# Two-layer graph network in fp32: W2 asked for behind x on one queue, adj of batch 2 handled within O of batch 1, the product WqWk in pieces of 128 columns

## The chip, the cores and the metric

The kernel runs on one core of a Trainium2 chip. The metric is the device time of one execution in microseconds (us), as a median of several executions. All timed executions here are marked as of the fast state, and only those are compared; one kernel was run once, and its state is unknown. The engines are called PE (tensor engine), PEld (its weight loads), DVE (vector engine), ACT (ScalarE), POOL (GpSimd) and SP (the engine that issues most of the DMAs). An *eviction* is the copy of a finished product out of PE's result memory; until it is done, the next product of the same buffer waits. The *granted clock* is the share of its full clock that PE was given.

## The reference

There are 32 independent batches of 512 x 512 fp32, with two layers. Cut to what matters:

```python
h = relu(layernorm(x))                                  # layer 0
agg = (adj @ h) / max(rowsum(adj), 1e-6)
x = x + relu(concat([h, agg]) @ W.T)                    # W = [W1 | W2]
h = relu(layernorm(x))                                  # layer 1
q, k = split(h @ Wqk); v = h @ Wv
w = (q * (adj @ (k * mask))).sum(-1) * mask / sqrt(512)
x = x + softmax(w)[:, :, None] * v
```

## The kernel before

Every product of 512 x 512 is done with seven block products (m1 to m7) in place of eight, and needs sums of blocks of both operands beforehand, on DVE. The products of a batch are y = h W2, o = h W1 + adj y (added to x), u = adj h1, t = h1 (Wq WkT), whose row sums with u give the softmax's scores, and v = h1 Wv. PE runs them in stages of 14 block products; O(1) is the stage of o of batch 1, and y(1)/u(0) the one that mixes y of batch 1 with u of batch 0. A stage has a *plan*: at each of its steps, other work is put behind the step's matmuls on the other engines. DVE and ACT keep to the order in which their instructions stand, so that one that waits holds up those behind it: in the trace before, ACT's scaling of adj waited 3.29 us, and the eviction behind it came at 100.41, while PE stood waiting for it.

```python
def multiply(d):                      # WqWk, once, between O of batch 0 and y(1)/u(0)
    p = held["m", d] = mm_tile(f"pm_{d}")
    for a in range(C):
        nc.tensor.matmul(p.rearrange("p a f -> p (a f)"), wqT[:, a, ts(d, P)], held["wkT"][:, a, :],
                         start=(a == 0), stop=(a == C - 1))
```

adj has to be scaled by its row sums and turned. It goes through DRAM: `sum` and `write` are ACT's, `degrees` is DVE's, `read` is a DMA that exchanges blocks, and `turn` is DVE's transpose of blocks of 32 x 32.

```python
class FrontA:
    def sum(self, c):      # ACT: row sums
        nc.scalar.activation(v, v, AF.Copy, accum_out=DEG[self.b][:, c:c + 1])
    def degrees(self, h):  # DVE: max and reciprocal
        ...
    def write(self, c):    # ACT scales, then a DMA to DRAM
        nc.scalar.activation(v, v, AF.Copy, scale=self.rdeg[:, c:c + 1])
        nc.sync.dma_start(out=self.to.d[c], in_=v)
class Turned:
    def read(self, h):     # four DMAs back from DRAM
    def turn(self, h):     # DVE transposes
    def sums(self, i):     # DVE: left sums of blocks
```

The start, and the plan of O of batch 0 as far as it turns the mask:

```python
def start():
    load_x(0)                                            # SP queue
    s2 = [exchange(weight_source(w0[:, F:2 * F])[8 * h:8 * h + 8], f"sw2_{h}", queue=nc.scalar) for h in range(2)]
    fa.load(0); fa.load(1)                               # adj of batch 0
    s1 = exchange(...)                                   # W1
    fh.load(0); sq = exchange(...); sk = exchange(...)   # x of batch 1, Wq, Wk
    ...                                                  # cut: layer norm of batch 0, y(0)
    fh.load(1); fb.load(0)                               # x and adj of batch 1
    nc.sync.dma_start(out=mask_sb, in_=nodemask)
    ...
    at(2, mask_order)                                    # DVE reorders the mask
    at(3, mask_turn)                                     # PE transposes it (pmk)
    at(4, mask_keep)                                     # ACT keeps it
```

## Time and profile before

| kernel before | value |
|---|---|
| time, median of 6 executions | 2382.48 us (2381.6 to 2383.76) |
| span of the profiled execution | 2380.0 us |
| PE busy | 99% |
| PE idle before its first instruction | 17.2 us |
| other PE waits of more than 0.15 us | 4, together 9.5 us, all between 97 and 148 us |

A PE that is 99% busy leaves 1% in question, and nearly all of that lies in the first 160 us. So the page's averages say little, and the timelines of these 160 us say nearly everything. They are shown in the prediction. Only the lines that are needed later for a comparison stand here. They are from the timelines of DVE (first) and PE (second; start, duration, instruction, count, and in brackets the idle time before it and what ended it):

```profile
11.49 0.69 DVE L221 BATCH_NORM_STATS2 st<-x 128x6 f32<-128x512 f32 x1 [10.63 <-DMA x<-in_x_dram]
```

```profile
17.23 1.97 PE L496 MATMUL h<-identity,h 128*128 128x128 f32 x8 [17.23 <-ACT h L533]
...
61.51 13.90 PE L645 MATMUL pm<-wkT,wqT 128*128 128x512 f32 x32
```

x is there at 11.5, PE begins at 17.2, and the product WqWk stands from 61.5 to 75.2 without a gap.

### The profile page before, as it was taken

The page shows a single profiled execution, that of the slowest core. Times are in us where ns is not written, and L with a number is a line of the kernel's source. Part 1 is how long each engine was busy: PE and PEld are TensorE (multiplying, and loading weights), DVE is VectorE, ACT ScalarE, POOL GpSimd, SP SyncE. Part 2 cuts the span into 40 slices and gives each one's busy share as a digit, 9 for nine tenths or more (in the row PEclk, how much of TensorE's full clock was granted, in tenths as well). Part 3 has the DMA queues.
Part 4 walks back from the last instruction along what each step waited for, and adds up shares of the span by engine and source line. Part 5 has one row for each costly group of instructions (what it writes and reads, how often), then busy time and mean ns, then how long its engine had stood idle before and what let it go on. Part 6 is the DMA issues. An engine that isn't in the chain of part 4 may idle for free.

```text
span 2380.0 us, 30871 instructions
## 1 busy us (share of the span) xinstructions
PE 2345.8 (99%) x10820; PEld 2056.2 (86%) x10820; DVE 1491.9 (63%) x3132; ACT 860.3 (36%) x1555; POOL 91.9 (4%) x134
## 2 busy tenths in 40 slices
PE   7999999999999999999999999999999999999998
PEld 6778888888888888888888888888888888888887
DVE  5666666666666666666666566666666666666544
ACT  4433333433333433334333334333343333343312
POOL 0000000000000000000000000000000000000000
PEclk9999999999999999999999999999999999999999
DMA  8845656456556456565465564565554565645412
GB/s 163 217 132 144 165 146 149 135 125 166 142 142 162 127 136 172 146 143 141 127 158 149 145 159 125 134 174 142 142 146 130 151 157 146 156 127 131 116 37 70
DMA packets 363596, 337.71 MB, mean 142 GB/s; under 512 B 32657, under 2 KB 266129, under 8 KB 363441
## 3 DMA queue, kind: packets, MB, share of 16 engines
q1 hardware_dynamic: 361264, 334.69, 55.8%
q10 hardware_dynamic: 2176, 1.05, 0.3%
q8 instruction: 85, 1.39, 0.3%
q14 instruction: 71, 0.57, 0.1%
HBM read 203.49 MB, written 132.12 MB: 141 GB/s over the span
## 4 chain that ended last, share of the span: by engine, by line
PE 95%; DMA 2%; DVE 1%; SPq 1%; ACT 0%; issue 0%; POOL 0%; DVEq 0%; ACTq 0%; POOLq 0%
PE pp_o L124 18%; PE pp_v L124 9%; PE pp_t L124 9%; PE pp_y L124 9%; PE pp_u L124 9%; PE pq_o L124 9%; PE pq_v L124 5%; PE pq_t L124 5%; PE pq_y L124 4%; PE pq_u L124 4%; PE pr_o L124 4%; PE pr_v L124 2%; PE pr_t L124 2%; PE pr_u L124 2%; PE pr_y L124 2%; DMA x<-in_x_dram 0%
## 5 line engine op out<-in xcount | busy, mean ns | idle before, releaser
L124 PE MATMUL pp_t<-mR,h1T 128*128 128x256 f32 x1024 | 243.8, 381 | 4.6 <-ACT t L91 4.6
L124 PE MATMUL pp_u<-h1m,aT 128*128 128x256 f32 x1024 | 242.0, 379 | 3.2 <-ACT u L91 3.2
L124 PE MATMUL pp_v<-vR,h1T 128*128 128x256 f32 x1024 | 242.0, 379 | 1.1 <-ACT v L91 1.1
L124 PE MATMUL pp_y<-w2R,hT 128*128 128x256 f32 x1024 | 243.0, 380 | 0.0
L124 PE MATMUL pp_o<-w1R,hT 128*128 128x256 f32 x1024 | 242.1, 379 | 0.5 <-ACT o L91 0.5
L124 PE MATMUL pp_o<-y,aT 128*128 128x256 f32 x1024 | 241.9, 379 | 0.0
L124 PEld LDWEIGHTS pp_t<-mR,h1T 128*128 128x128 f32 x1024 | 195.6, 191 | 31.8 <-ACT t L91 5.0
L124 PEld LDWEIGHTS pp_u<-h1m,aT 128*128 128x128 f32 x1024 | 194.5, 190 | 30.0 <-ACT u L91 3.6
L124 PEld LDWEIGHTS pp_y<-w2R,hT 128*128 128x128 f32 x1024 | 195.3, 191 | 27.1 <-issue 0.5
L124 PEld LDWEIGHTS pp_v<-vR,h1T 128*128 128x128 f32 x1024 | 194.5, 190 | 27.9 <-ACT v L91 1.5
L124 PEld LDWEIGHTS pp_o<-w1R,hT 128*128 128x128 f32 x1024 | 194.3, 190 | 27.2 <-ACT o L91 0.9
L124 PEld LDWEIGHTS pp_o<-y,aT 128*128 128x128 f32 x1024 | 194.5, 190 | 26.4
L91 ACT ACTIVATE o<-pp_o 128x512 f32<-128x512 f32 x96 | 57.3, 597 | 370.9 <-PE pp_o L124 370.9
L235 ACT ACTIVATE h1m<-x,nmr,rstd 128x512 f32<-128x512 f32 x128 | 100.0, 807 | 173.7 <-DVE nmr L231 173.7
L199 DVE STREAM_TRANSPOSE aT<-saT 128x1024 f32<-128x1024 f32 x62 | 77.2, 1245 | 130.1 <-DMA saT<-daT 102.1
L91 ACT ACTIVATE v<-pp_v 128x512 f32<-128x512 f32 x128 | 75.5, 590 | 223.3 <-PE pp_v L124 223.3
L91 ACT ACTIVATE y<-pp_y 128x512 f32<-128x512 f32 x128 | 76.4, 597 | 204.0 <-PE pp_y L124 204.0
L91 ACT ACTIVATE u<-pp_u 128x512 f32<-128x512 f32 x128 | 76.2, 595 | 140.4 <-PE pp_u L124 140.4
L227 POOL TENSOR_TENSOR rstd<-rstd,mhalf 128x4 f32<-128x4 f32 x64 | 66.6, 1040 | 1561.5 <-ACT m_o L91 879.8
L124 PE MATMUL pq_y<-w2R,hT 128*128 128x256 f32 x512 | 121.0, 379 | 0.0
L124 PE MATMUL pq_o<-w1R,hT 128*128 128x256 f32 x512 | 121.0, 379 | 0.0
L124 PE MATMUL pq_o<-y,aT 128*128 128x256 f32 x512 | 120.9, 379 | 0.0
(115 smaller groups left out, 3745.2 us busy)
## 6 DMA issues: line engine op xcount, KB each, us to landing
x<-in_x_dram SPq DMA_DIRECT2D x128, 256.0 KB, 5.8
a<-in_adj_dram SPq DMA_DIRECT2D x256, 128.0 KB, 3.1
dh1T<-h1m SPq DMA_DIRECT2D x128, 256.0 KB, 2.5
sh1T<-dh1T SPq DMA_DIRECT2D x256, 128.0 KB, 3.4
out_dram<-x SPq DMA_DIRECT2D x256, 128.0 KB, 2.3
n<-in_x_dram SPq DMA_DIRECT2D x248, 128.0 KB, 4.8
daT<-a SPq DMA_DIRECT2D x124, 256.0 KB, 2.0
dhT<-n SPq DMA_DIRECT2D x124, 256.0 KB, 2.0
```

What stands on the lines that cost most here:

```text
L91: nc.scalar.activation(o, i, AF.Copy)
L124: nc.tensor.matmul(p[:, rc, :], lt[:, LEFT[k], dk, ts(rc, P)], rt[:, RIGHT[k], dk, :], start=first and n == 0, stop=True, skip_group_check ...
L199: nc.vector.transpose(o, t.rearrange("p k (c r) -> p k c r", r=R))
L227: nc.gpsimd.tensor_tensor(rstd, rstd, mhalf, op=ALU.pow)
L235: nc.scalar.activation(o, i, AF.Relu, scale=t[1][:, c:c + 1], bias=t[2][:, c:c + 1])
```

## The change

Its intent has three parts. W2, which came over ACT's queue beside x, is asked for on SP's queue behind x, so that x comes sooner. The handling of batch 2's adj, which held DVE and ACT in the stages y(1)/u(0) and O(1), is spread over O(1), with its transposes late. WqWk is computed in pieces of 128 columns.

```diff
-        s2 = [exchange(weight_source(...)[8 * h:8 * h + 8], f"sw2_{h}", queue=nc.scalar) for h in range(2)]
+        s2 = [exchange(weight_source(...)[8 * h:8 * h + 8], f"sw2_{h}") for h in range(2)]
...
         def multiply(d):
             for a in range(C):
-                nc.tensor.matmul(
-                    p.rearrange("p a f -> p (a f)"), wqT[:, a, ts(d, P)], held["wkT"][:, a, :],
-                    start=(a == 0), stop=(a == C - 1),
-                )
+                for e in range(C):
+                    nc.tensor.matmul(
+                        p.rearrange("p a f -> p (a f)")[:, ts(e, P)], wqT[:, a, ts(d, P)],
+                        held["wkT"][:, a, ts(e, P)],
+                        start=(a == 0 and e == 0), stop=True, skip_group_check=True,
+                    )
...                                                       # stage y(1)/u(0)
-        at2(9, fc.sum, 0)
-        at2(10, fc.sum, 1)
-        at2(10, fc.degrees, 0)
-        at2(11, fc.write, 0)
-        at2(12, fc.write, 1)
         f3 = FH[3] = FrontH(3)
         at2(12, f3.load, 0)
-        at2(12, fc.to.read, 0)
-        at2(13, f3.load, 1)
...                                                       # stage O(1)
+                f, ta, th = FA[2], FA[2].to, FH[2].to
+                for h in range(2):
+                    for c in range(2):
+                        at(3 * h + c, f.sum, 2 * h + c)
+                        at(3 * h + c + 2, f.write, 2 * h + c)
+                    plan[3 * h + 2].insert(0, lambda h=h: FA[2].degrees(h))
+                    at(5 + 3 * h, ta.read, h)
+                    at(9 + 3 * h, ta.turn, h)             # before: steps 1 and 7
+                    at(10 + 3 * h, th.read, h)
+                at(4, FH[3].load, 1)
...                                                       # th.turn of batch 2: steps 3 and 4 of t(0)/v(0), before 1 and 2
...                                                       # the aT sums of batch 2 go to y(2)/u(1)
```

More of the change, by code (lines that the diff above doesn't have):

```diff
@@ L185, in half_rows, with exchange @@
         return t
-    def exchange(src, name, t=None, queue=None):
+    def exchange(src, name, t=None):
         if t is None:
@@ L192, in exchange @@
         for q in range(Q):
-            (queue or nc.sync).dma_start(out=t[q * R:(q + 1) * R, :, :], in_=src[:, :, ts(q, P)].rearrange("k r j -> r k j"))
+            nc.sync.dma_start(out=t[q * R:(q + 1) * R, :, :], in_=src[:, :, ts(q, P)].rearrange("k r j -> r k j"))
         return t
@@ L509, in start @@
         load_x(0)
-        s2 = [exchange(weight_source(w0[:, F:2 * F])[8 * h:8 * h + 8], f"sw2_{h}", queue=nc.scalar) for h in range(2)]
+        s2 = [exchange(weight_source(w0[:, F:2 * F])[8 * h:8 * h + 8], f"sw2_{h}") for h in range(2)]
         fa = FA[0] = FrontA(0)
@@ L724, in at @@
                 plan.setdefault(n, []).append(lambda: f(*args))
-            if i + 1 < B:
-                ta, th = FA[i + 1].to, FH[i + 1].to
-                n = 1 if i > 1 else 5
-                at(1, ta.turn, 0)
-                at(n + 2, ta.turn, 1)
-                at(3, th.read, 0)
-                at(n + 4, th.read, 1)
-                for k in range(4):
-                    at(n + 3 + k, ta.sums, k)
-            if i == 1:
-                for c in (2, 3):
-                    at(c - 2, FA[2].sum, c)
-                    at(c, FA[2].write, c)
-                plan[2].insert(0, lambda: FA[2].degrees(1))
-                at(3, ta.read, 1)
+            if i == 1:
+                f, ta, th = FA[2], FA[2].to, FH[2].to
[8 more added lines that the diff above has]
+                at(4, FH[3].load, 1)
                 for k in range(4):
@@ L744 @@
                     at(10 + k, F1[0].to.sums, k)
+            elif i + 1 < B:
+                ta, th = FA[i + 1].to, FH[i + 1].to
+                at(1, ta.turn, 0)
+                at(3, ta.turn, 1)
+                at(3, th.read, 0)
+                at(5, th.read, 1)
+                for k in range(4):
+                    at(4 + k, ta.sums, k)
             if i + 2 < B:
@@ L769 @@
             if i + 1 < B:
-                at(1, th.turn, 0)
-                at(2, th.turn, 1)
+                n = 1 if i > 1 else 3
+                at(n, th.turn, 0)
+                at(n + 1, th.turn, 1)
                 for k in range(4):
@@ L802 @@
             at(8, s.store, 1)
+            if i == 1:
+                for k in range(4):
+                    at(5 + k, FA[2].to.sums, k)
             t1 = F1[i].to
```

## The prediction

> **What bounds the kernel now.** I read the page first, for the bound. Then I read the tensor engine's waits, and then what lies behind each wait in the timelines of the vector engine (DVE), ScalarE (ACT) and the tensor engine (PE). The second column of a timeline is the duration, and the bracket holds the idle time before.
>
> ```profile
> PE 2345.8 (99%) x10820; PEld 2056.2 (86%) x10820; DVE 1491.9 (63%) x3132; ACT 860.3 (36%) x1555; POOL 91.9 (4%) x134
> ```
>
> PE is the bound. Nearly all its work is fp32 matmuls of 256 columns, whose instructions start every 0.216 us. From 161 us to the tail it has no recorded idle time, and the change touches nothing of the later loop passes. What can move is the start and the first 160 us, where all the waits lie:
>
> ```profile
> PE h L496 <- ACT h L533: 17.8, 2, 17.2
> PE pp_t L124 <- ACT t L91: 4.6, 1, 4.6
> PE pp_u L124 <- ACT u L91: 3.2, 1, 3.2
> PE pp_v L124 <- ACT v L91: 1.1, 1, 1.1
> PE pp_o L124 <- ACT o L91: 0.5, 1, 0.5
> ```
>
> The 17.2 us is the start: x lands (DVE's first statistics at 11.49), then the normalization, then the transposes. The other four sum to 9.5 us. Behind them stands DVE, held by the transposes of adj, and ACT behind DVE:
>
> ```profile
> 96.97 1.25 DVE L199 STREAM_TRANSPOSE aT<-saT 128x1024 f32<-128x1024 f32 x1 [3.43 <-DMA saT<-daT]
> 113.30 1.25 DVE L199 STREAM_TRANSPOSE aT<-saT 128x1024 f32<-128x1024 f32 x1 [7.36 <-DMA saT<-daT]
> 126.07 1.25 DVE L199 STREAM_TRANSPOSE aT<-saT 128x1024 f32<-128x1024 f32 x1 [5.41 <-DMA saT<-daT]
> ...
> 99.31 0.72 ACT L307 ACTIVATE a<-a,rdeg 128x512 f32<-128x512 f32 x1 [3.29 <-DVE rdeg L303]
> ...
> 115.49 1.33 ACT L307 ACTIVATE a<-a,rdeg 128x512 f32<-128x512 f32 x2 [8.35 <-DVE rdeg L303]
> ...
> 101.06 1.99 PE L124 MATMUL pp_u<-h1m,aT 128*128 128x256 f32 x8 [3.21 <-ACT u L91]
> ...
> 137.80 3.78 PE L124 MATMUL pp_t<-mR,h1T 128*128 128x256 f32 x8 [4.63 <-ACT t L91]
> ```
>
> The last two transposes of DVE are of adj of batch 2. In the first, ACT's scaling of that adj sits in front of the eviction that PE needs at 101. In the other two, DVE loses 12.8 us and reaches the h1T sums and the statistics late, so PE stands 4.63 us at 133.17. Its group at 137.80 then takes 3.78 us where its like takes 1.89:
>
> ```profile
> 120.00:140.00 20.00, 15.37 (x66) 13.08 (x66) 14.28 (x28) 4.00 (x6) 1.29 (x1) 0.92 0.45 137
> 140.00:160.00 20.00, 18.87 (x79) 15.92 (x79) 15.06 (x39) 8.86 (x15) 1.01 (x1) 0.91 0.50 143
> ```
>
> The column after POOL is the granted clock: in the trace it is 0.5 for 6.83 us from 136.68. PE ran 5.7 us of those and so lost about 2.85 us.
>
> **What the Trainium skill says.** (1) "TensorE: Matmul & The Clock Gate", Part 1 (the HAM clock gate): an idle window of about 3.4 us, free-running, halves the clock. The trace agrees: after 4.63 us idle the clock halved for 6.83 us; after 3.21 us idle it didn't. (2) The same page, LDWEIGHTS: a load costs columns / 1.2 ns, 107 ns for 128. The records show 190 ns each, but where two loads follow each other with nothing before them (44.13), they start 108 ns apart, and PEld's 0.30 us for both is 0.108 + 0.19. So 190 includes latency, and the trace agrees with 107 as occupancy. (3) "DMA: Bandwidth & Descriptors", Issuing engines are not separate DMA queues: queues share the same 16 DMA engines and interleave. The trace agrees: while x and W2 came by two queues, together they got 175 to 230 GB/s in each us from 4 to 12, no more than later loads from one queue. (4) The clock-gate page, "Architectural detail", calls ACT and DVE strict FIFO; the waits above, with evictions caught behind an unrelated adj operation, are that.
>
> **Part 1, W2 behind x.** Today x (four DMAs of 256 KB) shares the engines with W2 (1 MB in 512 B packets), and its fourth DMA is issued only at 4.73. It lands at 11.47. Alone at the front: the batch-1 x lands in steps of 1.1 us, and a first transfer of this size needs some 3.5 us (Wv: issued 54.23, landed 57.72), so 0.72 + 3.5 + 3 x 1.1 = 7.5; from the moved bytes (0.44 MB by 4 us, then 225 GB/s for 0.61 MB) 6.8. I take 7.2: x comes 4.3 us earlier. W2 needs 5.6 us after it (as W1's 1 MB did, 18.03 to 23.64) and lands at 12.8, just when DVE is through with the statistics. So y(0) starts about 4.3 us earlier, near 17.5.
>
> But the loads are saturated from 2 to 41 us, and changing their order doesn't make the sum smaller: by 13 us I count 2.28 MB moved before and 2.26 after. Last in that queue stands nodemask:
>
> ```profile
> 42.58 0.41 DVE L615 COPY mask_by<-mask 32x512 f32<-32x512 f32 x1 [1.96 <-DMA mask<-in_nodemask_dram]
> ...
> 43.77 0.43 PE L622 MATMUL pmk<-identity,mask_by 32*128 32x32 f32 x4
> ```
>
> The first line has DVE idle for the mask; PE arrives 0.74 us after DVE's copy is done (42.99 + 0.04 against 43.77). With the shift PE arrives at 39.5, waits for the mask until about 43.05, and of the 4.3 us only **0.7** are left. The gain turns into a new wait of 3.6 us. (W1 at 23.6 holds DVE for 1.8 us too, but PE meets w1R only at 32.)
>
> **Part 2, adj of batch 2 moved.** No work goes away. Two sums, a degrees step and two scalings leave the y(1)/u(0) stage; the second half's follow; the transposes move from O's steps 1 and 7 to steps 9 and 12; the four aT sums (4 x 0.6 = 2.4 us DVE) go one stage on, where DVE is busy 12 to 14 of 20 us.
>
> End of y(1)/u(0): the transpose at 96.97 (batch 1, stays) still holds DVE, but ACT no longer waits behind it: the eviction of u's c22 comes at 94.3 instead of 100.41. The **3.21** go.
>
> In O(1) I write times as after, O beginning near 99 (97.7 + 1.73, less 0.35). DVE clears its aT and y backlog at 104.5, gives the degrees at 106.0; ACT scales until 107.4; the loads in front keep the DMAs full until about 108, so the two writes land at 109.7. Then n of batch 3 is loaded (lands 113.9) and adj is read back (4 issues of 0.45, landing 116.2). DVE comes to that transpose at 115.5, so it waits 0.7 instead of 7.36. Second half: written by 116.9, read by 121.2, wanted at 122.2: no wait. DVE's work in O: 4 + 4 sums of mR and vR 4.8, finishes 4.3, statistics 3.2, transposes 2.5, h1T sums 2.4, small ones 1.0, so 18 us in a stage of 24.2. h1T's third sum is done at 124.0, PE needs it at 128.4; ACT's last normalization is done at 123.2, the first eviction of t is wanted at 125. So the waits of 0.5, 4.63 and 1.13 and the 2.85 of clock go: **9.1**. The narrowest place is v's m6 at 133.6, whose eviction stands behind a normalization that I put at 132.3: 1.3 us of slack.
>
> **Part 3, WqWk in pieces.** Before, 16 products x 2 instructions of 512 columns at 0.429 us are 13.73 us (61.51 to 75.24). After, 64 x 2 of 128 columns, each with a weight load of its own. Columns cost 0.107 + 0.0025, the load 0.107 in the shadow; transposes of 128 columns with a load each already start every 0.109. 128 x 0.1095 = 14.0, so **+0.3**, all on PE's path.
>
> **Sum**: 0.7 + 3.2 + 9.1 - 0.3 = 12.7 us off 2382.3, which gives 2369.6.
>
> **Rivals.** (a) *The start gain holds whole (4.3)*, if the mask lands earlier: 2366. For it: two queues interleaving may waste some bandwidth. Against: full DMA engines until 41 us. (b) *Loads can't be hidden at 128 columns*, so each instruction costs its recorded 190 ns: 128 x 0.19 = 24.3, +10.6, about 2380. For it: the records; against: the 108 ns and 109 ns spacings. I give it 7%. (c) *A wait takes the place of the ones removed*: adj's chain of write, load, read-back in O slips by over 2 us, DVE stands at step 9 or 12 and v's m6 waits 1 to 4 us: 2371 to 2374. For it: seven DMA steps in series, narrow slack; some 35%. (d) *The new mask wait halves the clock*: 3.6 us idle covers a free-running window of 3.4 in 5 to 20% of the phases, costing 1.7 to 3.4 us.
>
> **Range and chances.** Weighing (b), (c) and (d) with about 0.7, 0.7 and 0.4 us and (a) with -0.4 gives some 2371. The low end, 2366.5, is most of (a); the high end, 2376.5, is (c) with (d). Two per cent is 47.6 us; all the waits before the steady state, start included, are 27 us, so faster is all but excluded; slower would need something that I don't see.
>
> **What would show it.** x's statistics near 7.2; the first transposes near 13; a wait of about 3.6 us before pmk, at 43.0; weight loads of WqWk 0.11 us apart and its stage 14 us long; no wait at u's last product; the adj transposes of batch 2 near 116 and 122 with waits under 1 us; granted clock 1.0 from 120 to 160. It is wrong if WqWk takes over 20 us, if pmk comes before 41, or if t and v still wait more than 3 us.

## The result, and the profile after

The changed kernel takes 2368.66 us (median of 6 executions, 2365.43 to 2370.62), 13.8 us less than before in the same rounds. The ratio is 0.994, with a 95% interval of 0.9927 to 0.9953. Ratios here are the mean time of one kernel's fast runs over that of the other's of the same rounds, so they are not quite the ratio of the medians. By the measure of 2% it is "same".

PE's waits in the changed kernel (what waited, for what, us in total, times, longest), over the first 400 us:

```profile
PE h L496 <- ACT h L533: 14.2, 2, 13.7
PE pmk L622 <- DVE mask_by L615: 3.6, 1, 3.6
```

The four waits after 97 us are gone. (A stop too short for this list is left before 92.83, where a group starts 0.29 us late.) The start is 3.5 us shorter, and a wait of 3.6 us stands before the mask's transposes. The timelines of DVE (first) and PE (second) show where it comes from:

```profile
7.97 0.69 DVE L221 BATCH_NORM_STATS2 st<-x 128x6 f32<-128x512 f32 x1 [7.12 <-DMA x<-in_x_dram]
...
42.87 0.41 DVE L615 COPY mask_by<-mask 32x512 f32<-32x512 f32 x1 [6.29 <-DMA mask<-in_nodemask_dram]
```

```profile
13.71 1.97 PE L496 MATMUL h<-identity,h 128*128 128x128 f32 x8 [13.71 <-ACT h L533]
...
43.42 0.60 PE L622 MATMUL pmk<-identity,mask_by 32*128 32x32 f32 x4 [3.63 <-DVE mask_by L615]
43.96 3.36 PE L124 MATMUL pp_o<-w1R,hT 128*128 128x256 f32 x8
...
62.70 14.45 PE L646 MATMUL pm<-wkT,wqT 128*128 128x128 f32 x128
```

x lands 3.6 us sooner (its fourth DMA at 7.85 for 11.47). DVE then waits 6.29 us for the mask, which comes when it came before, and PE stands with it. The group at 43.96 takes 3.36 us where 1.89 is usual: the wait has halved PE's clock for 3.41 us. The windows show it (stretch, length, busy time of PE, PEld, DVE, ACT and POOL with counts, then the granted clock, the DMA share and GB/s), first for the kernel before, then for the changed one:

```profile
40.00:60.00 20.00, 20.00 (x96) 17.34 (x95) 14.31 (x29) 8.20 (x16) 1.01 (x1) 1.00 0.39 103
```

```profile
40.00:60.00 20.00, 16.57 (x72) 14.43 (x73) 12.54 (x25) 7.60 (x15) 1.01 (x1) 0.91 0.33 90
120.00:140.00 20.00, 20.00 (x95) 17.60 (x94) 18.96 (x37) 9.62 (x16) 2.29 (x2) 1.00 0.86 240
```

In the stretch from 120 to 140, where the kernel before had a PE of 15.37 and a clock of 0.92, PE now is busy throughout at full clock, and DVE is busy 18.96 of 20 us: it is nearly full there, but no longer in PE's way. The transposes of adj in DVE's timeline, first batch 1's second half and then the two of batch 2:

```profile
99.22 1.25 DVE L199 STREAM_TRANSPOSE aT<-saT 128x1024 f32<-128x1024 f32 x1 [3.36 <-DMA saT<-daT]
...
119.76 1.25 DVE L199 STREAM_TRANSPOSE aT<-saT 128x1024 f32<-128x1024 f32 x1 [1.59 <-DMA saT<-daT]
...
125.84 1.24 DVE L199 STREAM_TRANSPOSE aT<-saT 128x1024 f32<-128x1024 f32 x1
```

Of the 7.36 and 5.41 us that DVE stood before the last two, 1.59 are left.

The best single reading is a ledger. I took the starts of PE's groups at the borders of the stages in both timelines. The differences of neighbouring borders are what each stretch takes.

| stretch on PE | before | after | difference |
|---|---|---|---|
| start to the mask's transposes | 43.77 | 43.42 | -0.35 |
| mask's transposes to WqWk (end of O(0)) | 17.74 | 19.28 | +1.54 |
| WqWk | 13.73 | 14.29 | +0.56 |
| y(1)/u(0) | 27.65 | 24.57 | -3.08 |
| O(1) | 24.93 | 24.17 | -0.76 |
| t(0)/v(0) | 33.28 | 24.18 | -9.10 |
| from y(2) to the end | 2218.91 | 2218.85 | -0.06 |
| span | 2380.0 | 2368.8 | -11.2 |

The last stretch is 2218.9 us in every kernel of this study (2218.85 to 2218.95). So everything that any of them gains or loses lies before y(2). The profiled execution of the changed kernel is the slowest of its six. Why the others are up to 5 us faster is one of the questions below.

### The profile page after: what moved, and what is told of

Same layout as the page of the kernel before. It is cut to its first block, busy times and chain, and to the rows that moved or that the text cites. A ratio compares the mean times of both kernels' runs of the same rounds, so it can differ in the third digit from the quotient of the medians.

```text
span 2368.8 us, 31069 instructions
## 1 busy us (share of the span) xinstructions
PE 2343.9 (99%) x10916; PEld 2063.5 (87%) x10916; DVE 1491.9 (63%) x3132; ACT 861.2 (36%) x1555; POOL 91.9 (4%) x134
## 4 chain that ended last, share of the span: by engine, by line
PE 97%; DMA 1%; DVE 0%; ACT 0%; SPq 0%; POOL 0%; issue 0%; DVEq 0%; ACTq 0%
PE pp_o L124 19%; PE pp_v L124 9%; PE pp_t L124 9%; PE pq_o L124 9%; PE pp_u L124 9%; PE pp_y L124 9%; PE pq_v L124 5%; PE pq_t L124 5%; PE pq_y L124 5%; PE pq_u L124 5%; PE pr_o L124 5%; PE pr_v L124 2%; PE pr_t L124 2%; PE pr_u L124 2%; PE pr_y L124 2%; DMA n<-in_x_dram 0%
## 5 line engine op out<-in xcount | busy, mean ns | idle before, releaser
L124 PE MATMUL pq_t<-mR,h1T 128*128 128x256 f32 x512 | 121.0, 379 | 0.0
```

What stands on the lines that cost most here:

```text
L124: nc.tensor.matmul(p[:, rc, :], lt[:, LEFT[k], dk, ts(rc, P)], rt[:, RIGHT[k], dk, :], start=first and n == 0, stop=True, skip_group_check ...
```

## The experiments

My theory was that part 2 alone makes the gain, that part 1's gain is eaten by the wait for the mask, and that part 3 costs half a microsecond. Rivals were that the parts need each other, that the later waits swallow what part 1 or 3 does, and that a weight load that isn't hidden costs its recorded 0.19 us. Eight runs were made, one of them of the changed kernel once more; all gave correct results. "Before" in their rounds is 2382.32 us (25 executions) for the first four and 2382.35 us (9) for the last four.

### w2_alone: part 1 by itself

```diff
 # kernel before
-        s2 = [exchange(..., f"sw2_{h}", queue=nc.scalar) for h in range(2)]
+        s2 = [exchange(..., f"sw2_{h}") for h in range(2)]
```

> The kernel before with W2 put behind x on the one queue, nothing else. My theory: x lands near 7.9 us and the first transposes come near 13.7 as in the changed kernel, but the tensor engine stands some 3.6 us before the mask's transposes at 43, so the time is 2382.5 less 0.4, or plus 1.4 where that wait halves the clock: mean 2382 to 2383.5, with a wider spread than before's 2381.6 to 2383.8. The waits of 3.2, 0.5, 4.6 and 1.1 us later stay. Rival: the start gain holds, 2378 to 2379.

Measured: 2382.59 us (13 executions, 2381.32 to 2384.55), ratio 1.000 (0.9992 to 1.0008). PE's waits:

```profile
PE h L496 <- ACT h L533: 14.0, 2, 13.5
PE pp_t L124 <- ACT t L91: 3.8, 1, 3.8
PE pmk L622 <- DVE mask_by L615: 3.4, 1, 3.4
PE pp_u L124 <- ACT u L91: 2.7, 1, 2.7
PE pp_v L124 <- ACT v L91: 2.2, 1, 2.2
```

The start is 3.8 us shorter (17.8 to 14.0), and 3.4 us of it stand before the mask. Alone, part 1 gives nothing. The wider spread that was expected didn't come: it is 3.2 us, and that of the kernel before in the same rounds is 3.3 (2380.99 to 2384.32). In the profiled execution PE's clock was halved three times (at 43.6, 101.7 and 139.2), each time for 3.41 us, and WqWk began 1.1 us later than before (62.62 for 61.51).

### pieces_alone: part 3 by itself

```diff
 # kernel before, with multiply(d) of the changed kernel
-                    p..., wqT[:, a, ts(d, P)], held["wkT"][:, a, :],
+                        p...[:, ts(e, P)], wqT[:, a, ts(d, P)], held["wkT"][:, a, ts(e, P)],   # e in range(C)
```

> The kernel before with WqWk in pieces of 128 columns, nothing else. My theory: the product takes 14.3 us in place of 13.7 (128 instructions at 0.111), and the time goes up by 0.3 to 0.6 us, to 2382.8 to 2383.1. Rival: the later waits (3.2, 4.6 us) hang on transfers and on the vector engine, and swallow the longer product: no change, 2382.5, with those waits shorter by 0.5 us together.

Measured: 2382.73 us (13 executions, 2382.16 to 2383.87), ratio 1.0001 (0.9993 to 1.0009). The product took 14.29 us (61.10 to 75.39) for 13.73. PE's waits behind it:

```profile
PE pp_t L124 <- ACT t L91: 4.3, 1, 4.3
PE pp_u L124 <- ACT u L91: 2.9, 1, 2.9
PE pp_v L124 <- ACT v L91: 1.7, 1, 1.7
```

They sum to 8.9 us where the kernel before had 9.5 (one of 0.5 is gone, the others differ by 0.3 to 0.6). The cost of the product is plain, but 0.4 us of time lies within the noise, so how much of it the waits swallow isn't settled here. (The traces don't settle it either: in this one the clock halved once more than in the kernel before, at 101.9.) What the longer product costs where no waits stand behind it is measured in mask_later_512.

### adj_alone: part 2 by itself

```diff
 # changed kernel, with part 1 and part 3 undone
-        s2 = [exchange(..., f"sw2_{h}") for h in range(2)]
+        s2 = [exchange(..., f"sw2_{h}", queue=nc.scalar) for h in range(2)]
-                for e in range(C): ...                    # pieces of 128 columns
+                nc.tensor.matmul(p..., wqT[:, a, ts(d, P)], held["wkT"][:, a, :], ...)
```

> The kernel before with adj of batch 2 handled within O of batch 1, and nothing else. My theory: all of the gain is here. The four waits of 9.5 us and the halved clock from 136.7 to 143.5 (2.85 us) go: 2382.5 - 12.3 = 2370.2, within 1 us, with a small spread, since no wait of over 3 us is left after the start. Rival: the gain needed the start that comes earlier or the longer product as slack, then a wait of over 1 us comes back in O or in t and v: 2372 to 2376.

Measured: 2368.52 us (5 executions, 2368.28 to 2368.74), ratio 0.994 (0.9926 to 0.9953). The whole list of PE's waits is one line:

```profile
PE h L496 <- ACT h L533: 18.0, 2, 17.4
```

So part 2 alone gives 13.8 us, as much as the whole change, and the spread is 0.5 us. It needs neither the earlier start nor the longer product. The expected 12.3 us was the sum of the waits and of the clock. The stages show what was missing: from 75.11 to 147.62, y(1)/u(0), O(1) and t(0)/v(0) take 72.51 us where they took 85.86. That is 13.35, or 1.05 more than expected: a stop costs PE more than its idle time, as is worked out below.

### mask_later: nothing asks for the mask before it is there

```diff
 # changed kernel
-        at(2, mask_order)
-        at(3, mask_turn)
-        at(4, mask_keep)
+        at(8, mask_order)
+        at(9, mask_turn)
+        at(10, mask_keep)
```

> The changed kernel with the three steps that turn the mask moved from steps 2, 3, 4 of O of batch 0 to steps 8, 9, 10, so that nothing asks for the mask before it has landed. My theory: the wait of 3.6 us before the mask's transposes goes, and with it the halved clock after it that some executions have: 2365.5 (the changed kernel's best) - 3.6 = 2362, with a spread under 2 us. Rival: the next transfer of the same queue takes the wait over (adj of batch 1, landing at 42.7, or the loads for layer 1 near 80): 2365 or more.

Measured: 2365.67 us (5 executions, 2364.99 to 2366.22), ratio 0.9928 (0.9915 to 0.994). The whole list of waits, and the mask's transposes in PE's timeline:

```profile
PE h L496 <- ACT h L533: 14.0, 2, 13.5
```

```profile
50.38 0.43 PE L622 MATMUL pmk<-identity,mask_by 32*128 32x32 f32 x4
```

The mechanism is as the theory has it: no wait for the mask, no halved clock, and WqWk begins at 57.75, 4.95 us before the changed kernel's profiled execution. The expected 2362 was wrong, though, and not because another transfer took the wait over, for there is no other wait. It was wrong because I took 3.6 us off the *best* executions of the changed kernel. Against adj_alone, which has the late start and 512 columns, the kernel should gain 3.6 us of start and lose 0.56 of product, 3.0; it gained 2.85.

### after_again: why the changed kernel's executions spread over 5 us

The changed kernel unaltered.

> The changed kernel once more, to see why its six executions fall into two groups (2365.4 to 2367.3 and 2370.0 to 2370.6). My theory: the wait of 3.6 us before the mask's transposes covers a whole window of the clock gate in some executions and not in others; that alone makes 1.7 us (one halved window of 3.41 us), so the fast group must also have a shorter wait for the mask, 1 to 2 us less, from transfers that ran faster. Then the executions spread continuously from 2365 to 2371. Rival: two sharp groups, from the clock gate alone, 1.7 or 3.4 us apart.

Measured: 2367.83 us (5 executions: 2365.4, 2367.73, 2367.83, 2367.94, 2369.57). They fill the range between the former two groups. The traced one is of the middle:

```profile
42.63 0.40 PE L622 MATMUL pmk<-identity,mask_by 32*128 32x32 f32 x4 [1.37 <-DVE mask_by L615]
```

Its wait is 1.37 us, not 3.63, and the clock stays at 1.0. There are two causes. The mask landed at 42.05, not at 42.84. And PE came to it 1.5 us later (41.26 for 39.80): the trace has full clock first at 22.42, where the other has it at 19.46, so y(0) ran longer at half clock. The ledger accounts for the 2.7 us between the two spans: 0.79 up to the mask's transposes, 1.57 in what follows up to WqWk, where the other trace has the halved clock, and 0.40 in y(1)/u(0). Over all traces of this study the mask landed between 39.82 (adj_alone) and 42.84 us. An execution in which it lands before PE arrives would keep the whole gain of the start. (The earliest landing seen, 39.82, is just where PE arrives when its clock rises early.) And mask_later, whose trace has no such wait, lies at 2365.0 to 2366.2, just where the changed kernel's best ones lie (2365.40, 2365.43). I have no trace of one of those best executions, so for them this is inferred. Why the loads of one execution run up to 3 us ahead of another's stays open. It isn't the mask's own transfer alone: SP issued it anywhere from 36.18 (adj_alone) to 39.38 (the changed kernel), so the loads in front of it were already that far apart.

### mask_later_512: the mask later, and the product in pieces of 512 columns

```diff
 # mask_later, with multiply(d) of the kernel before
-                for e in range(C): ...                    # pieces of 128 columns
+                nc.tensor.matmul(p..., wqT[:, a, ts(d, P)], held["wkT"][:, a, :], ...)
```

> The kernel with W2 behind x, adj of batch 2 moved and the mask's three steps moved to 8, 9, 10 of O of batch 0, but WqWk in pieces of 512 columns as before. My theory: the product is 0.56 us shorter (13.73 for 14.29) and nothing behind it waits, so 2365.7 - 0.55 = 2365.1. Rival: the transfers of the stages behind are the bound and swallow it, 2365.7.

Measured: 2365.27 us (5 executions, 2364.69 to 2365.78), ratio 0.9929 (0.9915 to 0.9942). The ledger has WqWk at 13.74 us against mask_later's 14.29, and everything behind it is unchanged: from the end of WqWk to y(2) both take 72.52 us. So in the traces the product's 0.55 us are paid in full where no wait stands behind it. The medians differ by 0.4, which agrees, but the two kernels' executions overlap and are of different rounds, so the times alone don't show it. This is the lowest median of the study, 17.1 us under the kernel before of its rounds and 2.6 under the changed one of the same rounds.

### turns_late: which half of part 2 does what

```diff
 # changed kernel; sums, degrees and scalings of batch 2's adj back where they stood
+        at2(9, fc.sum, 0); at2(10, fc.sum, 1); at2(10, fc.degrees, 0)      # stage y(1)/u(0)
+        at2(11, fc.write, 0); at2(12, fc.write, 1); at2(12, fc.to.read, 0); at2(13, f3.load, 1)
...                                                                          # stage O(1)
-                        at(3 * h + c, f.sum, 2 * h + c)
-                        at(3 * h + c + 2, f.write, 2 * h + c)
-                    plan[3 * h + 2].insert(0, lambda h=h: FA[2].degrees(h))
-                    at(5 + 3 * h, ta.read, h)
-                at(4, FH[3].load, 1)
+                for c in (2, 3):
+                    at(c - 2, f.sum, c)
+                    at(c, f.write, c)
+                plan[2].insert(0, lambda: FA[2].degrees(1))
+                at(3, ta.read, 1)
                     at(9 + 3 * h, ta.turn, h)             # stays late
```

> The changed kernel, but the sums, degrees and scalings of batch 2's adj stand where they stood before (first half at the end of y(1)/u(0), second half at steps 0 to 3 of O), and only the two transposes stay at steps 9 and 12 of O. It tells apart the two halves of part 2. My theory: the wait of 3.2 us at u's last product comes back (ScalarE behind the degrees behind the transpose of batch 1's adj), with 0.15 for the restart; the waits in O, t and v don't. So 3.3 us above the changed kernel: 2369 to 2373.5, one wait of about 3 us at 100 us and none after. Rival: the late waits come back too, because ScalarE or the transfers carry them and not the blocked transposes: 2378 or more.

Measured: 2372.1 us (4 executions, 2371.76 to 2373.7), ratio 0.9958 (0.9944 to 0.9972), 4.3 us above the changed kernel of the same rounds. PE's waits after the start:

```profile
PE pp_u L124 <- ACT u L91: 2.4, 1, 2.4
PE pmk L622 <- DVE mask_by L615: 1.3, 1, 1.3
```

and the group behind the first of these:

```profile
99.25 2.67 PE L124 MATMUL pp_u<-h1m,aT 128*128 128x256 f32 x8 [2.35 <-ACT u L91]
```

The wait at u's last product is back, and none after it: the two halves do different things. Moving the sums and scalings away frees the eviction in y(1)/u(0); moving the transposes late frees O(1), t and v. (With the transposes went batch 2's aT sums and the read-back and turning of its h; what each of these does alone wasn't tested.) The rival falls. The wait is a little shorter than expected, but it halves the clock (2.67 us in place of 1.89, and O(1) is 25.23 us long in place of 24.17), which I hadn't expected of a stop of 2.35 us.

### pieces64: what a weight load costs when columns don't hide it

```diff
 # changed kernel
-                for e in range(C):
+                for e in range(2 * C):                    # columns ts(e, 64) in place of ts(e, 128)
```

> The changed kernel with WqWk in pieces of 64 columns: 256 instructions, each with its own weight load of 128 columns. It measures what a load costs when the columns no longer hide it. My theory: the load occupies 0.107 us, so the instructions start 0.107 to 0.112 us apart and the product takes 27.4 to 28.7 us, 14 more than the 14.3 of 128 columns. Rival: the record's 0.19 us is the cost once it isn't hidden, 48.6 us; or loads overlap each other, then 0.053 us apart and 14 us as before.

Measured, in one look: 2382.67 us (one execution, state unknown). The product in PE's timeline:

```profile
60.92 28.69 PE L646 MATMUL pm<-wkT,wqT 128*128 128x64 f32 x256
```

y(1) begins 28.53 us after the product does, so its 256 instructions are 0.1114 us apart on average. The 128 instructions of the changed kernel are 0.1116 us apart (14.29 us). With half the columns the pace doesn't change, so at 128 columns the load already is the limit, by a hair: 0.1116 us against 0.1073, a quarter of the 0.429 us that 512 columns take. A rival is a fixed cost of each instruction with its load, whatever they move. The mask's transposes speak against it: they too have a load each, and at full clock they start 0.06 us apart (43.859, 43.921 and 43.984 in the kernel before). The record of each load says 0.192 us in the changed kernel all the same.

## Why the prediction was right

The time of 2368.66 lies in the range of 2366.5 to 2376.5, 2.3 us below the 2371 predicted and 0.9 below the sum of 2369.6 before the rivals were weighed. The mechanisms of parts 1 and 2 were right; in part 3 the load, which should have been hidden, sets the pace. That the total came so near is partly luck: part 2 was put too low, what part 1 keeps was put too high and the cost of part 3 too low, and these errors cancel in part, in a kernel whose own executions spread over 5 us. By its own steps:

**Part 1, 0.7 us kept of 4.3.** The mechanism was right: the gain of the start turned into a wait for the mask, 3.63 us in the profiled execution against 3.6 predicted. Two sizes were off. x landed at 7.85, not 7.2: its DMAs landed 1.2 to 1.3 us apart and not 1.1, which alone makes 0.4 us, and the prediction had gone below its own 7.5 by a second reckoning. So the start was shortened by 3.5 us (17.23 to 13.71). And "until about 43.05" was taken as a fixed time. The transposes came at 43.42 in one trace of the changed kernel and at 42.63 in another. What was kept was 0.35 us in the first and 1.1 us in the second; w2_alone shows that by itself it is nothing that can be measured. One reading on the way was off: together x and W2 got 180 to 250 GB/s in each us from 4 to 12, not 175 to 230. The conclusion holds, with a mean of 204 before and of 199 in the changed kernel, which has one queue.

**Part 2, 3.2 and 9.1 us.** By the ledger the stage y(1)/u(0) gave 3.08, and would have given 3.48 (as in adj_alone) but for the small stop before 92.83; O(1), t and v gave 0.76 + 9.10 = 9.86 where 9.1 were predicted. The term that was too small is the stops themselves: the prediction added idle times, but the group that should start after 1.73 us started after 5.10 where PE's idle time was 3.21, so 3.37 were lost, and 0.66 where it was 0.50. The group behind a stop took 1.99 in place of 1.89, where the clock wasn't halved. So a stop cost 0.26 us beside its idle time, and four of them 1.04, which is what adj_alone gave beyond the 12.3 expected of it. adj_alone, with 13.8 us by itself, shows that nothing else was needed; turns_late shows both halves of the reason.

**The slack in O.** The transposes of batch 2 came at 119.8 and 125.8, not near 116 and 122. 2.5 us of that is the later begin of O(1) (101.56, predicted 99.07), which comes from the halved clock, the mask, the product and the small stop before 92.83; the rest is the chain of write, load and read-back, for which DVE waited 1.59 us and not 0.7. The place called the narrowest, v's m6, began at 136.09 with its eviction done at 135.21: 0.9 us of slack, predicted 1.3.

**Part 3, +0.3 us.** It is +0.56. The pace is that of the load, 0.1116 us, and not of the columns with 0.1095. Rival (b), 0.19 us each, is refuted by pieces64.

**Rivals.** (d), given 5 to 20%, came about in the execution that was profiled, and cost 1.54 us, a little less than its 1.7 to 3.4. There it went as (d) says: PE was idle from 39.80 to 43.42, which covers the window of the clock from 39.94 to 43.35. But a whole window isn't needed: one with 2.24 us idle was enough in turns_late. So 5 to 20% was too low for a wait that long. The mask's waits of 3.6 and 3.4 us (w2_alone) both halved the clock, and those of 1.3, 1.4 and 2.0 (turns_late, after_again, pieces64) didn't. (a) wasn't settled by the profiled execution. The best executions look like it (2365.4), without a trace to show it, and mask_later realizes it on purpose. (c) didn't come about.

**What remains open** is why the queue of start loads ends anywhere from 39.8 to 42.8 us.

## What to carry to other kernels

A transfer that is brought forward in a saturated queue gained here only until the next place that waits for a transfer of the same queue; list those places, and move the first use of the late ones (here three lines of plan, worth 2 to 3 us at the median) before reordering the loads. Where engines run in order, as DVE and ACT do here, an operation that waits for a DMA belongs late in the stream, behind whatever the bound engine will ask for: moving two transposes and their preparation made the kernel 13.8 us faster without removing any work. When you price a stop of the tensor engine, add its restart and look at where it falls in the clock's windows.

## What the Trainium skill lacked or had wrong

- "TensorE: Matmul & The Clock Gate", Part 1, says that full idle windows halve the clock, and its closing table warns of gaps over about 3 us. Where it speaks of shorter stops it gives no border. Here windows that were idle in part did it: taking the windows of 3.41 us from the clock's first change in each trace, halving followed windows with 2.09 us (pieces_alone), 2.24 us (turns_late, one stop of 2.35 us) and 2.69 us (w2_alone) idle, and didn't follow windows with 1.86 (w2_alone) and 1.92 us (before). The border lies between 56% and 61% in these traces.
- The same page, LDWEIGHTS, gives 107 ns for 128 columns. In a stream that the load bounds, fp32 loads came every 111 to 112 ns, and so did the instructions, of 128 and of 64 columns alike, while each load's record shows 192 ns, so that the record isn't the occupancy. And the loads of the mask's transposes, 128 columns of 32 partitions, came 59 to 64 ns apart in the kernel before, less than 107.
- No page tells how much the end of a saturated queue of loads varies between executions of closely related kernels: 39.8 to 42.8 us here for a queue that ends after 8 MB.
